# The order of the parts in a graph-attention kernel: logits of the first step in four single pieces instead of two pairs

## The chip, the cores and the metric

The kernel runs on one core of a Trainium2 chip. The metric is the device time of one execution in microseconds (us), lower is better. The kernel before takes 1484.36 us, the median of 3 runs (1482.55 to 1485.34).

Engines are named as in the profile: PE is TensorE's matrix unit and PEld its loading of weights, DVE is VectorE, ACT is ScalarE, POOL is GpSimd, SP is SyncE, which issues transfers.

## The reference, cut to what matters

One layer on a graph of 3327 nodes with 256 features. Each of two steps builds a dense attention matrix from the features, keeps in each row the largest entries until they hold 0.9 of the row's mass, and multiplies it with the features. Beside it runs a diffusion with a given sparse matrix.

```python
for n in range(2):
    q = Xa @ W1.T @ W2.T                 # 64 wide
    k = Xa @ W3.T
    probs = softmax(q @ k.T)             # 3327 x 3327: the logits, then exp
    # keep in each row the largest entries until their mass reaches 0.9
    A = probs * mask;  A = A / A.sum(-1)
    Xf = R @ Xf                          # R: adjacency + identity, rows scaled
    Xa = A @ Xa
    Z = Z + Xf @ U1[n].T + Xa @ U2[n].T
out = x + layernorm(X + Z)
```

Everything is float32. Rows are worked on in 26 tiles of 128, columns are padded to 3328.

## The kernel before

Each step is a software pipeline over the 26 row tiles. One turn of its loop is called a slot here. In a slot, different tiles are in different phases. Each phase is a Python generator, and each `yield` ends a portion of it. A plan, one string for each of seven parts of the slot (k0 to k6), says which generator goes on by one portion. The order of the text is the order of TensorE's, VectorE's and ScalarE's queues: dependences at the end of the program pin it.

The plan's letters, with the tile that each works on in slot i of the first step:

| letter | phase | tile | engines |
|---|---|---|---|
| m | estimate of the row's threshold, with two passes over the row | i+1 | ACT, then DVE |
| d | exact threshold and masking of the row (`settle`) | i | DVE |
| s | diffusion (`spread`) | i−2 | PE, DVE |
| e | end of the tile's first step, and preparation for the second (`first_end`, `prep`) | i−2 | PE, ACT, DVE |
| a | search of the adjacency for its entries (`listed`) | on its own | DVE, transfers |
| p, g | lists of entries, gathers | i+1, i | PE, ACT, DVE, POOL |
| q | queries of a tile and moments of its logits (first two portions of `weights`) | i+3 | PE, ACT, DVE, POOL |
| w | logits and exponentials (last four portions of `weights`) | i+2 | PE, ACT |

```python
def weights(step, t, live, known=True):
    qT, r["ms"] = yield from project(step, t, law=known)   # q: pq matmuls, copies qT and mq | yield
    yield                                                  # q: DVE's product over mq, then POOL
    w = HALF * P                          # 1664
    wd = w // CUT                         # 416: a quarter of the row, of both halves
    for n in range(CUT):                  # w: four pieces
        c = n * wd
        pl = ps_l.tile([P, 2, 512], F32, tag="pl", name="pl")      # two buffers
        for a in range(2):
            p = slice(a * DA, (a + 1) * DA)
            PE.matmul(pl[:, a, :wd], qT[p, :], keys[step][p]...[:, c : c + wd], start=True, stop=True)
        if n < CUT - 1:
            S.activation(e...[:, :, c : c + wd], pl[:, :, :wd], AF.Exp, accum_out=za[:, n : n + 1])
            yield
        else:
            ...                           # the same, the last column of the padding left out
```

The masked rows of the tile before are transposed four blocks at a time and multiplied with the features. This is done in every part of the slot, ahead of (`turn`) and behind (`sum`) the plan's letters:

```python
def turn(self, g, made):
    ...
    pt = ps_t.tile([P, 4, P], F32, tag="pt", name="pt")            # two buffers for all users of ps_t
    for j in range(w):
        PE.transpose(pt[:, j, :], e[:, (j0 + j) * P : (j0 + j + 1) * P], ident)
    eT = tpool.tile([P, 4, P], F32, tag="eT", name="eT", bufs=3)
    S.copy(eT[:, :w, :], pt[:, :w, :])

def sum(self, g):
    ...
    for c in range(4 * k, min(4 * k + 4, NT)):
        PE.matmul(self.pa, eT[:, c - 4 * k, :], self.xa[:, j, :], start=c == 0, stop=c == NT - 1)
```

`ps_t` has other users, each with its own buffer of the two in turn: the transposes of `xa` in `first_end`, `pk` and `pg` in `prep`, `pb` in `packed`, `po` in `gathered`, `pq` in `project`. Each is freed by a ScalarE copy.

```python
def first_end(t):                                   # letter e
    aT = transposed(live.pop(("r", t)))             # PE, copy xT | yield
    yield
    pz = ps_r.tile([P, 2 * D], F32, tag="pr", name="pz")
    for c in range(ND):
        PE.matmul(pz, aT[:, c, :], u2[:, c]..., start=c == 0, stop=c == ND - 1)
    S.copy(xw[:, t, :], pz[:, D:])
    sv = row.tile([P, D], F32, tag="sv", name="sv", bufs=2)
    V.tensor_tensor(sv, pz[:, :D], x0[:, t, :], ALU.add)
    ...
    yield
    yield from prep(1, aT, t)                       # pk, copies k and qry; of even tiles | yield, and pg, copy gt

def settle(step, t, r):                             # letter d
    V.scalar_tensor_tensor(w, e, col(16), e, ALU.is_lt, ALU.mult, accum_out=d2)     # L700
    ...                                             # 20 + 5 rounds of the 8 largest
    V.scalar_tensor_tensor(e, e, at(1), e, ALU.is_ge, ALU.mult, accum_out=ra)       # L734

# letter m, of the first step: ten small ACT operations | a pass over the row (L600) |
# a second pass (L600, "sign pass") | seven small ACT operations (L621 to L627) | DVE
# letter p: pb matmul, copy | DVE.     letter g: po matmul, copy lo | DVE, 10 gathers by POOL
```

The plan and the loop over it:

```python
PLAN = (("mdsssa", "mdsssa", "edawwp", "sda", "mpdea", "mdgawwq", "emdgq"), ...second step...)
...
for k in range(PARTS):                              # k0 to k6
    g = PARTS * (i - 1) + k - LATE[step]
    if summing:
        sums.turn(g, min(i, NT - 1))
    for c in "bb" + (... PLAN[0])[k]:
        next(work[c], None)
    if summing:
        ended = sums.sum(g)
        ...
for c in "cnwqsepgb" if step else "dmwqsepgb":      # what the plan left over
    run(work[c])
```

A second, general function in the same file searches the thresholds by bisection. It runs only where a check in the first finds a row wrong. The profile shows none of its lines.

Of the kernel before, what the change touches and what calls it, by code (L numbers as in the profile page):

```python
# [343 lines left out]
def guess_graph_layer(ctx, tc, x, adj, w1t, w2t, w3t, u1t, u2t, ln_g, ln_b, out, flag):  # L344
# [664 lines left out]
    def refetch(t):  # L1009
# [7 lines left out]

    PLAN = (("mdsssa", "mdsssa", "edawwp", "sda", "mpdea", "mdgawwq", "emdgq"),  # L1020
            ("cmss", "cnms", "wwnfd", "mdsss", "smwqdfg", "mqdfg", "mwdf"))

    LAST = {NT - 1: ("cfss", "cn", "ndddddd", "sss", "sf", "f", "f"), NT: ("cf", "v", "", "", "f", "f", "fv")}
# [4 lines left out]
    for step in range(2):  # L1028
        sums = Sums(step, live, xw if step else x0, AHEAD[step])

        for i in range(-1, NT + 2):
# [34 lines left out]
            for k in range(PARTS):  # L1066
                g = PARTS * (i - 1) + k - LATE[step]
                summing = valid(g // PARTS)
                if summing:
                    sums.turn(g, min(i, NT - 1))  # L1070
                for c in "bb" + (LAST.get(i, PLAN[1]) if step else PLAN[0])[k]:
                    next(work[c], None)
# [20 lines left out]
@with_exitstack  # L1093
def tile_graph_layer(ctx, tc, *args):
    keep = ctx.enter_context(tc.tile_pool(name="keep", bufs=1))
    flag = keep.tile([1, 1], I32, tag="flag", name="flag")
    guess_graph_layer(tc, *args, flag)
    failed = tc.nc.values_load(flag[0:1, 0:1], min_val=0, max_val=1 << 20)
    with tc.If(failed > 0):
        search_graph_layer(tc, *args)  # L1100
# [34 lines left out]
```

## Time and profile before

The profiled execution has a span of 1556.6 us, at a granted TensorE clock of 0.951. The first step's slots lie between some 180 and 845 us of it, the second step's between 925 and 1510.

| stretch | length, us | PE busy | DVE busy | ACT busy | POOL busy |
|---|---|---|---|---|---|
| first step, 380 to 845 us | 465.0 | 410.3 | 382.6 | 317.2 | 275.0 |
| second step, 925 to 1556 us | 631.0 | 547.7 | 551.2 | 516.1 | 492.2 |
| one slot of the second step | 23.54 | 21.36 | 21.11 | 20.79 | 20.63 |

The operations that the change touches:

| operation | line | mean ns | in all |
|---|---|---|---|
| logits `pl`, matmul record | L567 | 552 | 832 |
| exponential of a piece | L571 | 867 | 132 + 24 |
| transposes' copy `eT` | L781 | 555 | 364 |
| pass over a row, ACT | L600 | 3073 | 106 + 24 |

How to read the views: in a table by stage, busy time is given for each engine with the number of its instructions. In a list of waits, a row names who waited for whom, the sum in us, the times and the longest. In an order of time, a row has start, duration, engine, line, operation, output and inputs, how many were merged, and in brackets the idle time of the engine ahead of it and what ended it. A float32 matmul shows as two records, and records of neighbours overlap, so the start of the next row tells the pace.

### The profile page before, as it was taken

The numbers are of one execution on the slowest core, as the hardware profiler recorded it, in microseconds if no ns is written. First come the engines' busy times: TensorE is split into PE (matmuls) and PEld (weight loads), VectorE is DVE, ScalarE is ACT, GpSimd is POOL, SyncE is SP. The second block draws the span as 40 slices with busy tenths as digits, with TensorE's granted clock in tenths as the row PEclk, the third lists the DMA queues.
The fourth block names the chain that finished last, engine by engine and source line by source line (L and its number), as shares of the span: only waits on it lengthen the run. The fifth ranks groups of instructions, "written<-read, shape, count | busy, mean of one in ns | idle before, by whom it ended". The sixth has DMA issues, their size and how long they took to land.

```text
span 1556.6 us, 22648 instructions
## 1 busy us (share of the span) xinstructions
PE 1320.4 (85%) x6495; PEld 988.6 (64%) x6495; DVE 1230.2 (79%) x3837; ACT 1104.6 (71%) x2476; POOL 990.8 (64%) x1489
## 2 busy tenths in 40 slices
PE   5857888888888989979889937989989989998886
PEld 3523666666666667657667725767767667777675
DVE  4457797977988889779787238989888889898894
ACT  5537576676676676767665378988988988988961
POOL 6312555645756646556555156888888888888851
PEclk9978899999999999999999967999999999999998
DMA  7554343533533534434323131221221221222200
GB/s 220 167 163 134 105 139 96 152 105 96 156 109 107 143 105 116 127 106 130 114 65 89 53 88 31 72 79 55 72 75 49 81 67 57 82 65 59 82 18 20
DMA packets 97687, 149.81 MB, mean 96 GB/s; under 512 B 15985, under 2 KB 60528, under 8 KB 97552
## 3 DMA queue, kind: packets, MB, share of 16 engines
q1 hardware_dynamic: 78400, 104.00, 21.7%
q0 software_dynamic: 16640, 42.69, 10.6%
q10 hardware_dynamic: 2512, 1.57, 0.3%
q8 instruction: 54, 0.88, 0.2%
q14 instruction: 81, 0.66, 0.2%
HBM read 120.93 MB, written 27.28 MB: 95 GB/s over the span
## 4 chain that ended last, share of the span: by engine, by line
PE 34%; POOL 23%; ACT 20%; DVE 9%; issue 7%; DMA 4%; another core or an unknown queue 1%; SPq 0%; POOLq 0%; ACTq 0%; DVEq 0%
PE pa L793 15%; ACT ja L600 8%; POOL xg L868 7%; PE pt L779 4%; POOL g L678 4%; PE pr L876 4%; PE pl L567 4%; DMA at<-in_adj 3%; ACT e L571 3%; PE pz L889 2%; ACT eT L781 2%; DVE e L734 1%; PE pk L487 1%; DVE cand L705 1%; POOL rstd L468 1%
## 5 line engine op out<-in xcount | busy, mean ns | idle before, releaser
L781 ACT COPY eT<-pt 128x512 f32<-128x512 f32 (+1 forms) x364 | 201.8, 555 | 226.2 <-PE pt L779 145.9
L793 PE MATMUL pa<-xw,eT 128*128 128x256 f32 x1352 | 331.8, 387 | 29.2 <-ACT xa L800 28.6
L793 PE MATMUL pa<-x,eT 128*128 128x256 f32 x1352 | 348.2, 401 | 5.6 <-ACT eT L781 4.5
L859 POOL DMA_INDIRECT ac<-in_adj,index x130 | 176.7, 1359 | 249.2 <-DVE mq L541 152.3
L600 ACT ACTIVATE ja<-e,g 128x3328 uint8<-128x3328 f32 x106 | 325.8, 3073 | 0.1
L793 PEld LDWEIGHTS pa<-xw,eT 128*128 128x128 f32 x1352 | 250.0, 191 | 91.9 <-ACT xa L800 33.3
L793 PEld LDWEIGHTS pa<-x,eT 128*128 128x128 f32 x1352 | 258.7, 199 | 59.9 <-issue 14.5
L705 DVE MAX8 cand<-w 128x8 f32<-128x168 f32 (+1 forms) x1040 | 251.2, 317 | 0.0
L779 PE MATMUL pt<-ident,e 128*128 128x128 f32 x1144 | 179.9, 278 | 39.5 <-DVE e L734 22.9
L868 POOL DMA_INDIRECT xg<-bx,index x130 | 165.9, 1276 | 47.6 <-issue 33.4
L779 PEld LDWEIGHTS pt<-ident,e 128*128 128x128 f32 x1144 | 143.6, 144 | 79.0 <-issue 32.5
L567 PE MATMUL pl<-k,qT 64*128 64x416 f32 x832 | 186.2, 552 | 4.5 <-ACT qT L531 4.0
L700 DVE SCALAR_TENSOR_TENSOR w<-e,g 128x3328 f32<-128x3328 f32 x44 | 163.9, 3725 | 0.7
L876 PE MATMUL pr<-xg,ac 128*128 128x257 f32 (+1 forms) x520 | 138.6, 390 | 22.8 <-DVE s L1003 20.2
L868 POOL DMA_INDIRECT xg<-vx,index x130 | 128.2, 986 | 44.0 <-issue 35.1
L811 DVE TENSOR_REDUCE fm<-at 128x4 f32<-128x512 f32 (+1 forms) x182 | 115.8, 637 | 49.2 <-DMA at<-in_adj 47.3
L734 DVE SCALAR_TENSOR_TENSOR e<-e,rec 128x3328 f32<-128x3328 f32 x40 | 147.4, 3684 | 0.0
L571 ACT ACTIVATE e<-pl 128x832 f32<-128x832 f32 x132 | 113.4, 867 | 7.5 <-PE pl L567 6.9
L876 PEld LDWEIGHTS pr<-xg,ac 128*128 128x128 f32 x520 | 91.0, 195 | 33.6 <-DVE s L1003 20.5
L567 PEld LDWEIGHTS pl<-k,qT 64*128 64x128 f32 x832 | 71.0, 189 | 51.0 <-issue 41.2
L712 DVE MAX8 bb<-cand 128x8 f32<-128x160 f32 x286 | 92.7, 324 | 6.4
L892 DVE TENSOR_TENSOR sv<-pz,x 128x256 f32<-128x256 f32 x26 | 11.0, 422 | 91.4 <-ACT xw L890 81.2
(226 smaller groups left out, 2213.5 us busy)
## 6 DMA issues: line engine op xcount, KB each, us to landing
at<-in_adj SPq DMA_DIRECT2D x156, 256.0 KB
cx<-ac SPq DMA_DIRECT2D x26, 384.0 KB
ac<-cx SPq DMA_DIRECT2D x26, 384.0 KB
bx<-e SPq DMA_DIRECT2D x26, 128.5 KB
own<-bx SPq DMA_DIRECT2D x26, 128.5 KB
x<-in_x SPq DMA_DIRECT2D x13, 256.0 KB
xr<-in_x SPq DMA_DIRECT2D x26, 128.0 KB
ax<-e SPq DMA_DIRECT2D x26, 128.0 KB
```

The source lines that it names most:

```text
L567: PE.matmul(pl[:, a, :wd], qT[p, :], keys[step][p].rearrange("p a b -> p (a b)")[:, c : c + wd], start=True, stop=True)
L571: S.activation(e.rearrange("p (a n) -> p a n", a=2)[:, :, c : c + wd], pl[:, :, :wd], AF.Exp, accum_out=za[:, n : n + 1])
L600: S.activation(ja, e, f, bias=guess, scale=sign, accum_out=total)
L700: V.scalar_tensor_tensor(w, e, col(16), e, ALU.is_lt, ALU.mult, accum_out=d2)
L705: V.max(cand[:, 8 * s : 8 * s + 8], w[:, s * SEG : min(NP, (s + 1) * SEG)])
L734: V.scalar_tensor_tensor(e, e, at(1), e, ALU.is_ge, ALU.mult, accum_out=ra)
L779: PE.transpose(pt[:, j, :], e[:, (j0 + j) * P : (j0 + j + 1) * P], ident)
L781: S.copy(eT[:, :w, :], pt[:, :w, :])
L793: PE.matmul(self.pa, eT[:, c - 4 * k, :], self.xa[:, j, :], start=c == 0, stop=c == NT - 1)
L859: G.indirect_dma_start(out=ac[:, k, :], out_offset=None, in_=rows, in_offset=bass.IndirectOffsetOnAxis(ap=index[:, t, k : k + 1], axis=0), ...
L868: G.indirect_dma_start(out=xg[:, k, :w], out_offset=None, in_=rows, in_offset=bass.IndirectOffsetOnAxis(ap=index[:, t, k : k + 1], axis=0))
L876: PE.matmul(pr[:, :w], ac[:, k, :], own if k == KT - 1 else xg[:, k, :w], start=k == 0, stop=k == KT - 1)
```

## The change

Only the plan of the first step changes. The two pairs `ww` in k2 and k5 become single `w` in k2, k3, k5 and k6. The letter `q` goes out of the plan; its two portions then run at the end of the slot with what is left over (after `d`, `m` and `w`). The letter `e` gets a fourth place: `prep`'s `pk` moves from k6 to k5, and `pg` from the end of the slot to k6. Within k2, `e` and now `w` and `p` stand ahead of `d` and `a`. The purpose is to spread the logits' matmuls and exponentials evenly over the slot.

```diff
-    PLAN = (("mdsssa", "mdsssa", "edawwp", "sda", "mpdea", "mdgawwq", "emdgq"),
+    PLAN = (("mdsssa", "mdsssa", "ewpda", "wsda", "mpdea", "mwedga", "wmdeg"),
             ("cmss", "cnms", "wwnfd", "mdsss", "smwqdfg", "mqdfg", "mwdf"))
```

## The prediction

> **What bounds the kernel now.** I read the busy table first, then the waits, then the order of time of single engines inside one slot.[...]
>
> ```profile
> PE 1320.4 (85%) x6495; PEld 988.6 (64%) x6495; DVE 1230.2 (79%) x3837; ACT 1104.6 (71%) x2476; POOL 990.8 (64%) x1489
> ```
>
> No engine is full, and three are near it. So I cut the first step into slots, each from one `w<-e,g` of VectorE (L700) to the next. The columns are the stretch, its length, the busy time of PE, PEld, DVE, ACT and POOL, the granted clock, the DMA share and GB/s.
>
> ```profile
> 383.55:409.67 26.12, 21.99 (x115) 16.58 (x115) 23.50 (x72) 19.25 (x46) 20.77 (x24) 1.00 0.45 131
> 409.67:440.77 31.10, 27.62 (x136) 21.27 (x137) 24.14 (x79) 20.37 (x51) 15.43 (x22) 0.95 0.38 111
> 440.77:466.41 25.64, 23.16 (x120) 17.36 (x119) 24.08 (x81) 19.28 (x46) 20.23 (x23) 1.00 0.44 129
> ```
>
> VectorE needs some 24.1 us of every slot, 25.1 with the short steps between its instructions (440.77 to 466.41 is 25.64 with a single wait of 0.63). A slot cannot be much shorter than that. The long slots are long because ScalarE stands still for 2 to 6 us ahead of one `eT` copy, and VectorE then waits for `xw`. The waits of 330 to 845 us:
>
> ```profile
> ACT eT L781 <- PE pt L779: 64.2, 37, 6.2
> DVE sv L892 <- ACT xw L890: 54.7, 8, 7.5
> PEld pq L526 <- ACT eT L781: 41.7, 18, 3.5
> PEld pk L487 <- ACT mq L535: 23.1, 15, 2.6
> PEld pb L832 <- ACT eT L781: 6.0, 10, 0.6
> ```
>
> The first two are the stall. Its transposes are long done when it happens: the copy at 723.21 belongs to transposes that start at 718.66. I take it for something that the recording adds, because the profiled run is 1558.33 us and the timed ones 1484.36, and 74 us over 26 slots is 2.8 us a slot, the size of the stall. That is a choice, not a finding. The last three waits are real dependences: each names an operation whose PSUM buffer (`ps_t`, two buffers) is held by the ScalarE copy named beside it.
>
> Now one slot in order of time on the tensor engine, from k0's transposes (702.12) to k4's (714.78):
>
> ```profile
> 702.12 0.60 PE L779 MATMUL pt<-ident,e 128*128 128x128 f32 x4
> ...
> 708.65 0.38 PE L476 MATMUL pt<-ident,xa 128*128 128x128 f32 x2
> 708.96 1.67 PE L567 MATMUL pl<-k,qT 64*128 64x416 f32 x8
> 710.56 0.38 PE L832 MATMUL pb<-over,upto 128*128 128x1 f32 x2
> 710.80 1.97 PE L793 MATMUL pa<-x,eT 128*128 128x256 f32 x8
> ...
> 714.78 0.60 PE L779 MATMUL pt<-ident,e 128*128 128x128 f32 x4
> ```
>
> No row there has an idle time in brackets: TensorE is dense from k0 to k4, 12.66 us. ScalarE in the same stretch:
>
> ```profile
> 702.75 0.59 ACT L781 COPY eT<-pt 128x512 f32<-128x512 f32 x1 [1.63 <-PE pt L779]
> ...
> 706.70 3.08 ACT L600 ACTIVATE ja<-e,g 128x3328 uint8<-128x3328 f32 x1
> 709.67 0.20 ACT L600 ACTIVATION_READ_ACCUMULATOR ja<-e,g 128x1 f32 x1
> 709.76 0.58 ACT L781 COPY eT<-pt 128x512 f32<-128x512 f32 x1
> ...
> 713.25 0.59 ACT L781 COPY eT<-pt 128x512 f32<-128x512 f32 x1 [0.88 <-issue]
> ```
>
> It is dense from 702.75 to 712.3 and waits for TensorE afterwards. So the first half is TensorE's; in the second half ScalarE sets the pace (copy, sign pass, small operations, exponentials), and TensorE waits for it.
>
> [...]at 723.85 `pq` waits 2.87 us for `eT`, and the sum behind it, whose operand had been ready since 715.47 + 0.59, waits too. So a blocked operation delays all behind it, and where a piece stands in the text decides.[...]
>
> **The change, part by part.** It adds and removes no instruction; it moves them. A piece is four matmuls in eight records, (710.56 − 708.96) / 2 = 0.80 us of TensorE, and one exponential of 0.85 us on ScalarE (`e<-pl`, mean 867 ns).
>
> *First half.* The second piece moves from k2, ahead of `pb`, to k3, behind the transposes. `pb` takes the third `ps_t` buffer in k2 (transposes, `xa` transposes, `pb`), and there are two, so it waits for the first copy of k2 on ScalarE: 709.76 + 0.58 = 710.34, and some 0.1 more until TensorE starts. Before, TensorE reaches `pb` at 710.46, just when it comes free (the table has 0.6 us at most for it). After, it reaches it at 708.96 + 0.80 = 709.76 and stands still until 710.45: 0.7 us. The sum starts at about 710.7 as before, but the second piece, 0.8 us, still has to be done in k3. k4's transposes, and ScalarE's chain behind them, come **0.7 us later**. Nothing on ScalarE could move forward: it is dense from 702.75 on.
>
> *Second half.* Call the start of k4's transposes T. From 748.97 on the trace has ScalarE's chain without a gap. Counted from k4's copy (T + 0.69): sign pass 0.48, `xw` 3.55, k5's copy 3.80, seven small operations 4.28 to 6.63, `lo` 6.65, third piece 6.70, fourth 7.55, `qT` 8.53, `mq` 8.68, and TensorE's `pk` at 9.03, that is T + 9.72. Then `pk` and the last sum take 2.28, so the next k0 is at T + 12.0; in a slot of an even tile, with 0.39 more in `pk` and `pg`, at about T + 12.75 (728.44 to 731.52 is 3.08).
>
> After the change TensorE does: transposes, `pz`, sum, transposes (until T + 4.32), third piece (5.15), `pk` (5.7), `po` (5.9), sum (7.7). k6's transposes need the buffer of `pk`, which ScalarE frees after k5's copy, the small operations and the third piece: about T + 8.9, a wait of 1.2 in place of `pk`'s 0.9. Then transposes 0.24, fourth piece 0.83, sum 1.73, `pq` 0.55: next k0 at T + 12.25. For an even tile `pk`'s extra work lies in the wait and `pg` follows the fourth piece: about T + 12.6. So **+0.25 and −0.15 us in alternate slots, nothing on average**.
>
> *The end of the slot.* `q` no longer stands in the plan, so both its steps run behind everything else, and VectorE's square of `mq` comes directly behind TensorE and ScalarE (T + 12.8). VectorE's next `w` starts at about T + 13.1 instead of 12.7. That ties VectorE to the others once a slot, but it is not late for them.
>
> *Sum.* The cycle of TensorE and ScalarE is 12.66 + 12.0 or 12.75, mean 25.05 us, and becomes 25.75. VectorE's own cycle is 25.1. While the two were equal, some of any wait was hidden, so I count 0.4 of the 0.7 us: 26 slots × 0.4 = **10 us slower, 1494 us**. The second step keeps its plan and 23.54 us a slot.
>
> **Rivals.** (1) *Spreading pays*: the pieces fill TensorE's waits in the second half, and `pq`'s wait for k5's copy (41.7 us in the table) disappears. For it: `pq` no longer stands in k5, and `pk` can run while ScalarE is busy. Against it: `po` waits for the same copy, and the new wait ahead of k6's transposes is as long as the old one. If it paid in full, 0.8 us a slot, it would give about 1465. (2) *VectorE is the bound, all is hidden*: its 25.1 us a slot speak for it, the idle 6 us in every second slot against it. It would make 1484. (3) *The lock at the end costs more*: if VectorE must wait for `mq` in every slot and then brings `xw`'s user and the masking of `e` late, a whole 1 us a slot is lost: 1510.
>
> **Range and chances.** The full 0.7 us in 26 slots is 18 us (1502), and with the third rival up to 1518; a gain of half the first rival gives 1474. I take 1472 to 1518 for 8 in 10. Faster by over 2% (under 1455) would take 1.1 us a slot of gain, for which I find no place: 0.04. Slower by over 2% (over 1514) takes 1.15 us a slot: 0.14. The rest, 0.82, is within 2%.
>
> **What would show it.** The profile after should have a wait of about 0.7 us of `pb` for `eT` in nearly every slot; a wait of `pt` L779 for the `k`, `qry` copies of about 1.2 us in place of `pk` for `mq`; no more `pq` for `eT`, and no gap ahead of `po` larger than before; 12.66 us from k0 to k4 grown to about 13.3; VectorE waiting for `mq` at the end of most slots. I am wrong if the slot hangs on VectorE alone, if the stall that I take for the recording's is in the timed runs and moves with the order[...].

## The result, and the profile after

The changed kernel takes **1508.9 us** (median of 4 runs, 1507.08 to 1511.44), the kernel before 1484.85 us beside it (4 runs, 1482.55 to 1486.2). The ratio is **1.0165, with a 95% interval of 1.0144 to 1.0186**. It lost 24 us where the prediction has 10, inside its range of 1472 to 1518.

The busy table of the kernel after, with the same columns as before:

```profile
PE 1325.3 (88%) x6495; PEld 972.2 (64%) x6495; DVE 1229.5 (81%) x3837; ACT 1113.0 (74%) x2476; POOL 971.8 (64%) x1489
```

The profile of before in the prediction has a span of 1556.6 us, so this table can't be set against it. I therefore took a second profile of the unchanged kernel, called "before again" from here on (it is also the first experiment):

```profile
PE 1296.0 (87%) x6495; PEld 980.9 (66%) x6495; DVE 1231.2 (83%) x3837; ACT 1104.7 (74%) x2476; POOL 1014.4 (68%) x1489
```

The span grew from 1484.9 us to 1509.7, and the busy time of PE by 29.3, although it has the same 6495 matmuls. VectorE has not more to do. So the matmuls have become dearer, or stand differently; no work was added.

The table by stage of the kernel after, two slots of the first step, each from one L700 to the next (length; busy time of PE, PEld, DVE, ACT, POOL; clock; DMA share; GB/s):

```profile
558.78:585.45 26.67, 25.69 (x132) 18.77 (x131) 23.39 (x72) 20.24 (x50) 17.12 (x25) 1.00 0.48 130
585.45:611.86 26.41, 24.97 (x126) 18.11 (x125) 24.10 (x79) 20.04 (x48) 15.70 (x22) 1.00 0.46 129
```

And two of before again, first a long one, then one of the usual length:

```profile
339.02:365.55 26.53, 23.98 (x128) 18.40 (x127) 24.12 (x79) 19.20 (x47) 16.47 (x22) 1.00 0.48 136
...
596.92:622.16 25.24, 24.23 (x129) 18.71 (x129) 24.31 (x79) 19.56 (x49) 16.48 (x22) 1.00 0.50 139
```

After, the slots alternate like clockwork, 26.4 and 26.7, and PE is busy in all but 1.0 to 1.4 us of each. Before, they vary from 24.9 to 26.9 (between 240 and 740 us), and the long one is not long for PE's work: PE is busy for 23.98 us, less than in the short one, and stands still for 2.6. The mean slot is 25.68 us before again and 26.55 after: +0.87 us, and 26 × 0.87 = 22.6 us. That is nearly the whole loss. The second step, from the start of its first L700 to the end of its last, takes 588.73 us before again and 589.62 after. The granted clock is 1.00 in the four slots shown (over the whole span it is 0.962 before again and 0.960 after) and plays no part.

The waits of the kernel after, 330 to 845 us (who waits for whom: sum in us, times, longest):

```profile
DVE mq L541 <- ACT mq L535: 21.1, 17, 2.0
PEld pt L779 <- ACT qry L497: 20.6, 18, 1.4
PEld pb L832 <- ACT eT L781: 19.2, 17, 1.1
```

The three waits that the prediction named are there: `mq`, `pt` for `qry`, `pb` for `eT`. The wait of `pk` for `mq`, 23.8 us in 19 times in before again (240 to 760 us), is gone. So is the wait of `pq` for `eT`, but that is not the change's doing: before again hasn't got it either. The 41.7 us of it in the prediction's list belong to the stalled profile.

One slot of the kernel after, on the tensor engine in order of time (start, duration):

```profile
584.72 0.66 PE L779 MATMUL pt<-ident,e 128*128 128x128 f32 x4
...
591.61 0.97 PE L567 MATMUL pl<-k,qT 64*128 64x416 f32 x4
593.04 0.38 PE L832 MATMUL pb<-over,upto 128*128 128x1 f32 x2 [0.46 <-ACT eT L781]
...
595.10 0.60 PE L779 MATMUL pt<-ident,e 128*128 128x128 f32 x4
595.62 0.97 PE L567 MATMUL pl<-k,qT 64*128 64x416 f32 x4
596.52 1.99 PE L793 MATMUL pa<-x,eT 128*128 128x256 f32 x8
598.36 0.60 PE L779 MATMUL pt<-ident,e 128*128 128x128 f32 x4
...
607.31 0.44 PE L779 MATMUL pt<-ident,e 128*128 128x128 f32 x2 [0.98 <-ACT qry L497]
607.67 0.97 PE L567 MATMUL pl<-k,qT 64*128 64x416 f32 x4
608.57 1.99 PE L793 MATMUL pa<-x,eT 128*128 128x256 f32 x8
610.50 0.49 PE L526 MATMUL pq<-qry,w2d 64*128 64x128 f32 x2
610.82 0.39 PE L528 MATMUL pq<-qm,qry 64*128 64x130 f32 x2
611.14 0.66 PE L779 MATMUL pt<-ident,e 128*128 128x128 f32 x4
```

From k0 to k4 it is 598.36 − 584.72 = 13.64 us, where the prediction has 13.36 (12.66 + 0.7). The single piece of k3 takes 596.52 − 595.62 = 0.90 us, not 0.80, and its neighbours are longer too: transposes 0.52 (595.62 − 595.10), sum 1.84 (598.36 − 596.52). In the same part of before again these are 0.43 (606.80 − 606.37) and 1.73 (608.53 − 606.80), with no piece between.

The loads of weights at that place in the kernel after:

```profile
594.88 0.58 PEld L779 LDWEIGHTS pt<-ident,e 128*128 128x128 f32 x4
595.62 0.30 PEld L567 LDWEIGHTS pl<-k,qT 64*128 64x128 f32 x4 [0.17 <-issue]
596.52 1.59 PEld L793 LDWEIGHTS pa<-x,eT 128*128 128x128 f32 x8 [0.60 <-issue]
```

This is where the extra time sits. The transposes' weights (`128*128`) are loaded 0.22 us before their matmul (594.88 and 595.10). The logits' weights, half as high (`64*128`, called half-height below), and the sum's behind them, `128*128` again, come only with their own matmul (595.62 and 596.52), after 0.17 and 0.60 us in which PEld did nothing. So the first load is pulled ahead of its matmul, and the two at these changes of shape are not.

The same holds throughout. I took every change from one operation to the next on PE between 240 and 760 us, in before again and after. Where both loads are `128*128` and PE shows no wait, the second starts 0.03 to 0.43 us ahead of its matmul in 662 of 664 cases (the other two are `pz`, which depends on VectorE), and the matmul's record overlaps the one before it by 0.14 to 0.16 us. At every change to or from another shape, 102 in before again and 204 after, the load comes with its matmul (0.00 us ahead), and the records overlap by 0.07 us where PE doesn't wait. Half the width (`128*64`) does it too: `pg`, at 621.29 in both views of before again, is one of them.

```profile
621.29 0.19 PEld L502 LDWEIGHTS pg<-krs 128*64 128x64 f32 x2 [0.33 <-issue]
```

From `pl` to `pq` in before again, both `64*128`, the load is 0.35 us ahead. So it is the change of shape that costs, some 0.09 us of PE each time (0.16 − 0.07), and neither half the height as such nor a change of operation. Before again has 4 such changes in odd slots and 6 in even ones, after has 10 and 11.

### The profile page after: what moved, and what is told of

It reads as the page before. It is cut to its first block, busy times and chain, and to the rows that moved or that the text cites. A ratio compares the mean times of both kernels' runs of the same rounds, so it can differ in the third digit from the quotient of the medians.

```text
span 1509.7 us, 22676 instructions
## 1 busy us (share of the span) xinstructions
PE 1325.3 (88%) x6495; PEld 972.2 (64%) x6495; DVE 1229.5 (81%) x3837; ACT 1113.0 (74%) x2476; POOL 971.8 (64%) x1489
## 3 DMA queue, kind: packets, MB, share of 16 engines
q1 hardware_dynamic: 78400, 104.00, 22.6%
## 4 chain that ended last, share of the span: by engine, by line
ACT 33%; PE 24%; POOL 23%; DVE 8%; issue 7%; DMA 5%; SPq 0%; ACTq 0%; POOLq 0%; DVEq 0%
ACT ja L600 15%; PE pa L793 11%; POOL xg L868 7%; ACT eT L781 5%; POOL g L678 4%; PE pt L779 4%; PE pl L567 4%; DMA at<-in_adj 3%; ACT e L571 3%; PE pz L949 1%; POOL rstd L468 1%; DVE fm L811 1%; DVE cand L705 1%; POOL xr L906 1%; POOL g L677 1%
## 5 line engine op out<-in xcount | busy, mean ns | idle before, releaser
L793 PE MATMUL pa<-x,eT 128*128 128x256 f32 x1352 | 333.5, 388 | 1.5 <-ACT eT L781 1.5
L793 PEld LDWEIGHTS pa<-x,eT 128*128 128x128 f32 x1352 | 247.9, 191 | 69.8 <-issue 35.9
L859 POOL DMA_INDIRECT ac<-in_adj,index x130 | 133.3, 1026 | 187.6 <-DVE index L852 138.9
L567 PE MATMUL pl<-k,qT 64*128 64x416 f32 x832 | 199.0, 563 | 5.3 <-ACT qT L531 4.8
L868 POOL DMA_INDIRECT xg<-bx,index x130 | 151.3, 1164 | 48.5 <-issue 31.6
L700 DVE SCALAR_TENSOR_TENSOR w<-e,g 128x3328 f32<-128x3328 f32 x44 | 163.9, 3725 | 0.7
L811 DVE TENSOR_REDUCE fm<-at 128x4 f32<-128x512 f32 (+1 forms) x182 | 115.7, 636 | 44.9 <-DMA at<-in_adj 44.5
L567 PEld LDWEIGHTS pl<-k,qT 64*128 64x128 f32 x832 | 66.6, 187 | 48.0 <-issue 38.0
L949 PE MATMUL pz<-u,xw 128*128 128x512 f32 x104 | 59.3, 700 | 17.5 <-DVE e L952 14.7
```

Of the source, the lines that this page charges most:

```text
L567: PE.matmul(pl[:, a, :wd], qT[p, :], keys[step][p].rearrange("p a b -> p (a b)")[:, c : c + wd], start=True, stop=True)
L859: G.indirect_dma_start(out=ac[:, k, :], out_offset=None, in_=rows, in_offset=bass.IndirectOffsetOnAxis(ap=index[:, t, k : k + 1], axis=0), ...
L868: G.indirect_dma_start(out=xg[:, k, :w], out_offset=None, in_=rows, in_offset=bass.IndirectOffsetOnAxis(ap=index[:, t, k : k + 1], axis=0))
```

## The experiments

The theories before them: **A**, TensorE's chain of one slot is longer, by the wait of `pb` and by what the split costs in the second half; **B**, VectorE is locked to the others at the end of the slot, now that `q` runs last (the prediction's third rival). A further question was why a chain that grows by over 1 us shows less than that in the time.

**Before again, each half alone, and `q` earlier.** The first is the unchanged kernel. The next two take one half of the change. The last takes the changed kernel and lets `q` run ahead of the last sum, so that VectorE gets `mq` earlier.

```diff
 before           "edawwp", "sda",  "mpdea", "mdgawwq", "emdgq"
 after            "ewpda",  "wsda", "mpdea", "mwedga",  "wmdeg"
+first half alone "ewpda",  "wsda", "mpdea", "mdgawwq", "emdgq"
+second half alone "edawwp", "sda", "mpdea", "mwedga",  "wmdeg"
+q earlier        "ewpda",  "wsda", "mpdea", "mwedga",  "wmdegqq"
```

> The kernel before, unchanged, profiled once more. If the 2 to 6 us stalls of ScalarE in every slot of the first step were the recording's: a span near the timed 1485 us, slots of 25.4 to 25.7 us, no stall. If they belong to the kernel: a span near 1556 us again and slots of 28 and 30 us in turn.

> Only the first half of the change: the first pair is split over k2 and k3, the second pair and q stay as before. Theory A (TensorE's wait ahead of pb and its changes between kinds of matmuls lengthen the chain of TensorE and ScalarE): k0 to k4 takes 13.6 us as after the change, the whole some 16 us more than before, 1500. Theory B (the loss is VectorE's wait for mq at the end of the slot, since q left the plan): q is where it was, so 1485 to 1488.

> Only the second half: the second pair is split over k5 and k6, pk moves to k5 and q to the end of the slot; the first pair stays. Theory A: k0 to k4 takes 12.7 us as before, k4 to the next k0 12.8 to 13.0; 8 us more than before, 1493. Theory B: the whole loss, 1505 to 1509, with VectorE waiting 1.5 us for mq in every slot.

> The changed plan, with q ahead of the last sum of the slot, so that pq and mq come 1.9 us earlier and VectorE need not wait for mq. Theory A: the chain of TensorE and ScalarE is as long as before this edit, 1505 to 1511, and VectorE waits the same time elsewhere (for xw). Theory B: the loss goes, 1485 to 1490.

From the traces I took the start of k0's and k4's transposes on PE in every slot of the middle of the step. T is k4's; "odd" and "even" are the two kinds of slot, as in the prediction.

| kernel | k0 to k4, us (odd / even where they differ) | k4 to next k0, odd / even, us | mean slot, us | time, us | ratio to before, 95% |
|---|---|---|---|---|---|
| before again | 12.71 / 12.66 | 12.08 / 12.88 | 25.68 | 1486.59 | (one run) |
| after | 13.63 | 12.78 / 13.03 | 26.55 | 1508.9 | 1.0165 (1.0144 to 1.0186) |
| first half alone | 13.63 / 13.58 | 12.07 / 12.88 | 26.09 | 1498.16 | 1.0081 (1.0064 to 1.0097) |
| second half alone | 12.71 | 12.78 / 13.03 | 25.62 | 1486.26 | 1.0004 (0.9995 to 1.0013) |
| `q` earlier | 13.58 | 12.50 / 12.93 | 26.30 | 1504.67 | 1.0125 (1.0107 to 1.0143) |

(The third column is that of slots in which PE does not wait for VectorE; before again and the first half alone also have longer ones.) Three things follow.

*The stall belongs to the first profiled execution alone.* Before again has none: the largest wait of VectorE for `xw` between 240 and 760 us is 1.4 us, and the span is that of the timed runs.

*On the chain the halves add.* The first costs 0.92 us, the second 0.70 in odd slots and 0.15 in even ones, and the kernel after has both. The chain goes from (12.71 + 12.08 + 12.66 + 12.88) / 2 = 25.17 to 13.63 + (12.78 + 13.03) / 2 = 26.54 us: **+1.37**.

*In the time they don't.* The second half alone costs nothing that the interval can see (−0.5 us), the first 11.4 us, both 24. Before, the chain is 0.5 us shorter than the slot of 25.68, so something else fills those 0.5 us. The second half alone uses them up: its chain is 12.71 + (12.78 + 13.03) / 2 = 25.62, and that is its slot.

*The lock falls.* With `q` earlier VectorE hardly waits for `mq` any more. Its waits in that kernel, 240 to 760 us:

```profile
DVE sv L892 <- ACT xw L890: 21.1, 17, 4.0
...
DVE mq L541 <- ACT mq L535: 2.3, 12, 0.2
```

In the kernel after, the same stretch has 26.3 us for `mq` (20 times) and 4.5 for `xw`. The wait moved to `xw`, and only 4.2 us of 24 came back (5.9 by the ratios). PE's own pace accounts for them: its first part of the slot is 0.05 us shorter and its second 0.19 in the mean of odd and even, which is 26 × 0.24 = 6.2 us. The second half alone says the same from the other side: it too runs `q` last, VectorE waits 11.6 us for `mq` in 17 slots, and the time is that of before. And the first half alone leaves `q` where it was and still has half of the loss.

This run also measures the changes of shape. In odd slots `pq`, half-height too, now follows the last piece directly, and the sum runs behind both: two changes of shape fewer, with the same operations and the same wait for `qry` (0.98 us). The slot is 0.28 + 0.05 = 0.33 us shorter. In even slots `pg` still stands between, and there is one change fewer: 0.10 + 0.05 = 0.15 us.

**The wait of `pb` taken away.** `pb` moves to k3, where a buffer is free. Once in the kernel after, once in the first half alone:

```diff
 after                          "ewpda", "wsda",  "mpdea", "mwedga",  "wmdeg"
+after, pb later                "ewda",  "wpsda", "mpdea", "mwedga",  "wmdeg"
+first half alone, pb later     "ewda",  "wpsda", "mpdea", "mdgawwq", "emdgq"
```

> The changed plan with p (pb) moved from k2 to k3, behind the second piece, where the buffer it takes has long been freed. Theory A: pb's wait of 0.63 us a slot goes, the dearer single pieces stay: k0 to k4 takes 13.0 us instead of 13.63, slots of 25.8 to 26.0, 1491 to 1496. Rival (the wait at pb is only slack, ScalarE is late anyway): 1505 to 1510.

> Only the first pair split over k2 and k3, and pb moved behind the second piece, so that it doesn't wait. Theory A: what is left is the price of a single piece among full-width matmuls, 0.29 us: k0 to k4 13.0 us, the chain 25.5 us, which is under what VectorE takes with its waits (25.67), so 1484 to 1489. Rival (a split first pair costs what the run with the first half alone showed, pb or not): 1496 to 1500.

The times are 1498.22 us (ratio 1.0094, 1.0071 to 1.0117) and 1490.56 (1.0041, 1.0025 to 1.0058), both above what I expected. From k0 to k4 it is 13.1 us in both: 0.53 less than after, and still 0.4 more than before. So the wait of `pb` is 0.53 of the first half's 0.92 us, and 0.4 are left when nobody waits. The waits of 240 to 760 us show what is left. In before again:

```profile
DVE fm L811 <- DMA at<-in_adj: 13.1, 14, 1.8
PEld pb L832 <- ACT eT L781: 12.6, 21, 0.6
PEld pa L793 <- issue: 9.6, 40, 0.2
```

In the first half alone with `pb` later:

```profile
PEld pa L793 <- issue: 21.5, 60, 0.6
...
PEld pb L832 <- ACT eT L781: 12.0, 20, 0.6
```

The row of `pb` is the same although its buffer has long been free here. So these 0.6 us are not a wait for the copy, as the prediction read them, but the late load behind a half-height piece. (In the kernel after, the row has 1.1 us at most: the same 0.6, and 0.53 of real wait.) The sum's load of weights waits 20 times more, one in each slot, and 11.9 us more, 0.6 each time: the load that is not pulled ahead behind the lone piece of k2. In the kernel after it is 26.9 us and 69 times: 29 more than before, which is one in k3 of every slot and one in k6 of every second (in even slots `pg` stands between the piece and the sum).

In the middle of the step the slots are as expected: 26.0 us in the kernel after with `pb` later, which is its chain, and 25.7 in the first half with `pb` later, the slot of before, so that there the 0.4 us are hidden. The miss lies mostly at the start: by 240 us of the span both runs are some 3.5 us behind before again. Why is open.

**VectorE more work.** If VectorE fills the 0.5 us, more work on it must show in the kernel before nearly in full, and in the kernel after only beyond the time that it stands idle. Three more searches of the 8 largest (0.35 us each, 1.05 us a slot), ahead of the real one that overwrites their results, so the output is the same:

```diff
+ for _ in range(3 * (step == 0)):
+     V.max(bb[:, 1:9], cand)
```

> The kernel before with three more MAX8 over the candidates for each row tile of the first step, 1.05 us of VectorE a slot, whose results are overwritten. Theory A (VectorE sets the slot of the kernel before, which is what hid part of the change's cost): 20 to 28 us slower, 1505 to 1513. Rival (TensorE and ScalarE set it already): 0 to 6 us slower.

> The changed kernel with the same 1.05 us of VectorE a slot. Theory A: it fits into the 1.4 us that VectorE waits for mq in each slot, 1508 to 1514. Rival (VectorE's end of the slot is what makes the change slow): 20 us or more slower, 1530.

Before with it takes 1507.19 us (ratio 1.0151, 1.0126 to 1.0177): +21.6, or 0.83 us a slot for 1.05. **VectorE's work is on the path of the kernel before**, with PE's chain 0.5 us shorter. After with it takes 1521.09 (1.0231, 1.0197 to 1.0264), +12 (10 by the ratios) where I expected at most 5. Its four runs spread from 1516.28 to 1531.04 us, and the profile is that of the slowest, so its waits are larger than those of a middle run. VectorE's waits there, 240 to 760 us (its lines stand two further down, so L813 is L811):

```profile
DVE fm L813 <- DMA at<-in_adj: 29.1, 19, 2.9
```

These are all of them; the waits for `mq` are gone. After has no such wait for `at` at all, before again 13.1 us. The spare time was used up, and waits for loads came on top. That VectorE's later work delays these loads is a guess: in the kernel before, the same extra work left the waits for `at` as they were (13.0 us, 14 times).

How VectorE's lateness reaches PE, in a long slot of before again. First VectorE, then PE:

```profile
350.28 0.69 DVE L811 TENSOR_REDUCE fm<-at 128x4 f32<-128x512 f32 x1 [1.48 <-DMA at<-in_adj]
...
351.08 0.48 DVE L1003 SCALAR_TENSOR_TENSOR s<-pr,rrs,s 128x256 f32<-128x256 f32 x1
```

```profile
351.62 1.98 PE L889 MATMUL pz<-u,xT 128*128 128x512 f32 x4 [1.54 <-DVE s L1003]
```

VectorE waits 1.48 us for a load of the adjacency, brings the diffusion's product `s` late by that, and `pz`, whose PSUM buffer `s` has to free, waits 1.54 us. In the table by stage this is the hole in PE's long slots. After, PE is slower, it has no wait for VectorE between 240 and 760 us, and the hole is gone.

**The loads earlier, and ScalarE's copies first.** Two attempts to make the kernel before faster. In the first, the store of `cx`, which stands ahead of those loads in SyncE's queue, moves to behind the store of `vx`; also in the kernel after. In the second, k5's letters are turned so that its two short copies go first; and both together.

```diff
-    nc.sync.dma_start(cx[t], ...)
     yield
     ...                              # the store of vx
+    nc.sync.dma_start(cx[t], ...)
```

```diff
-"edawwp", "sda", "mpdea", "mdgawwq", "emdgq"
+"edawwp", "sda", "mpdea", "gqwwmda", "emdgq"
```

> The kernel before, with the store of ac to cx issued behind the store of vx in spread, so that its wait for the gathers doesn't hold up the loads of at behind it in SyncE's queue. Theory A: VectorE's waits for at (13 us in all) and TensorE's for VectorE go; slots of 25.16 us, the chain's own, 1471 to 1479. Rival (the loads are late for another reason): 1482 to 1488.

> The changed kernel with the same move of the store. Theory A: no change, its chain of TensorE and ScalarE takes 26.54 us whatever VectorE does: 1506 to 1511, so that the distance to the kernel before with the same move is some 35 us. Rival (VectorE and its loads set the changed kernel too): it falls as the kernel before does.

> The kernel before with k5 as gqwwmda: po and pq ahead of the logits' pair, and the copies lo, qT and mq and both exponentials ahead of the seven small operations, so that pk finds its buffer free. Theory A: k4 to the next k0 shrinks from 12.08 and 12.88 to some 11.7 and 12.3 us, but VectorE with its waits for at sets the slot: 1478 to 1486. Rival (VectorE doesn't set it): 26 times 0.45 us less, 1473.

> Both: the later store and po, pq and the copies first. Theory A: VectorE's work alone, 25.1 us a slot, is what is left: 1469 to 1476. Rival (the later store brings nothing): as with the copies first alone.

The store later: 1484.14 us (1.0003, 0.9993 to 1.0014), no gain, a miss. The queue of SyncE waits as before, at the moved store (in before again 176.9 us, 21 times, the longest 13.7):

```profile
SPq L1004 <- DMA ac<-in_adj,index: 177.0, 21, 13.6
```

VectorE's wait for `at` only fell from 13.1 to 10.4 us. Since the queue is held up as long as before, this run can't tell whether that hold-up makes the loads late. After with it: 1507.01 (1.0152, 1.0126 to 1.0177), unchanged, as expected, since VectorE has time to spare there.

Copies first: 1484.8 (1.0016, 1.0003 to 1.0029). PE's second half falls as low as 11.48 us in odd slots, 0.6 less than before. In even slots it is never under 13.02 between 260 and 740 us, because PE waits for VectorE's `s` in each of them (0.49 to 1.94 us). Nothing is gained. The waits of 240 to 760 us have the reason:

```profile
DVE fm L811 <- DMA at<-in_adj: 14.4, 14, 2.1
...
PE pz L889 <- DVE s L1003: 13.8, 13, 1.9
```

In before again the second is 7.5 us, 7 times. **A shorter chain of PE only waits longer for VectorE.** Both together give 1484.43 (1.0004, 0.999 to 1.0018), where I expected 1469 to 1476. No kernel of the study is faster than the kernel before.

## Why the prediction was off in size

- *The stall is the recording's*: right in that the timed runs are without it, as is the second profile of the same kernel. That the recording made it is not shown; the first profiled execution was itself that slow (1558.33 us).
- *The three real waits of the list*: only that of `pk` for `mq` is one. That of `pq` for `eT` went with the stall, so the first rival had nothing to gain there, and the 0.6 us of `pb` are a late load behind a half-height piece.
- *First half, the wait of `pb`*: right in place and kind. `pb` waits in every slot, and taking the wait away gives 0.53 us of the predicted 0.7 back. TensorE starts 0.05 us after the copy ends (593.04 against 592.42 + 0.57), where the prediction has some 0.1.
- *First half, the second piece*: wrong in size. It was counted at half a pair's 0.80 us. It costs 1.09 (from k3's transposes to k4's, 2.17 us grow to 3.26): of the difference about 0.10 is the piece itself, 0.09 the transposes ahead of it and 0.11 the sum behind it. With 0.1 more in k2 the first half is 0.92, not 0.7. (The prediction's "four matmuls in eight records" are the pair; a piece is two matmuls in four records. Its 0.80 us is half of the pair's time and isn't touched by that.)
- *Second half, k6's transposes*: right. They start at T + 8.95 in the slot shown (607.31 − 598.36), predicted at 8.9, and wait 0.98 us for `qry` on PE, predicted 1.2.
- *Second half, from there to k0*: **the step that failed with the most weight.** The prediction has 0.24 + 0.83 + 1.73 + 0.55 = 3.35 us. Measured in that order: 0.36 + 0.90 + 1.93 + 0.64 = 3.83 (607.67 − 607.31, 608.57 − 607.67, 610.50 − 608.57, 611.14 − 610.50). Every term stands beside a change between half-height and full-height matmuls and is dearer for it; the prediction priced these matmuls as if their neighbours didn't matter. So +0.25 and −0.15 became +0.70 and +0.15.
- *VectorE and `mq`*: right. VectorE waits at the end of nearly every slot, and it isn't late for what follows.
- *The sum*: predicted +0.7 us on the chain, 0.4 of them visible. Measured: +1.37, 0.87 visible. The term that was mis-sized is the price of the changes of shape. Before has two groups of half-height matmuls in a slot (a pair; a pair with `pq`), after has five (four pieces and `pq`). That is three more, and when the 0.53 us of `pb` are taken from 1.37, 0.84 us are left, **0.28 for each** in the mean. They are not equal: 0.40 for the one of the first half, 0.70 for the two of the second in odd slots, and 0.15 in even ones, where the wait ahead of k6's transposes is 0.5 us shorter (0.51) than `pk`'s was (1.01) and takes up the rest. The hidden share was held as 0.3 us and is 0.5: VectorE's cycle was taken as 25.1 us, without its waits for loads, and the slot is 25.68.
- *The rivals*: spreading does not pay, since the wait ahead of k6's transposes took the place of `pk`'s and `pq` had none to lose. VectorE as the bound is half true: it sets the slot of before, and PE's chain that of after. The third rival came nearest in time, 1510, and its cause is not the one at work.

What is open: that loads come late at a change of shape is shown, and that merging two groups gives the time back; why the hardware does not pull these loads ahead is not. What keeps the loads of `at` late in the kernel before is not found; the gathers that SyncE's queue waits for are a candidate that one moved store did not test.

## What to carry to other kernels

When work is spread more finely, count the changes of shape on the engine and not only the work: here three more groups of half-height matmuls cost TensorE as much as one whole piece of logits (0.84 us a slot in the mean; a piece in a pair takes 0.80). Where two engines each fill the slot, measure one chain and one slot apart: here they are 25.17 and 25.68 us, the second half alone made the chain 0.45 us longer for free, and the copies first, up to 0.6 us shorter in odd slots, gained nothing. Look for the difference with a little useless work on the engine that you suspect (1.05 us of VectorE a slot cost 0.83 here), and profile the unchanged kernel twice before its waits are explained.

## What was not expected of the hardware

- Two half-height float32 matmuls standing alone cost 1.09 us of TensorE's pace and 0.80 in a pair. In the two traces no load is pulled ahead at a change of shape (306 changes: 102 before again, 204 after), to half the width as to half the height.
- One profile of a kernel had stalls of 2 to 6 us a slot and a span of 1556.6 us, the next profile of the same kernel none and 1484.9.
- More work on VectorE in the kernel after (1.05 us a slot) went with 29.1 us of waits for loads, 19 times, in the slowest of four runs, where the kernel after has none.
